# Seven block products for the left multiplication of two gated steps, scalings on ScalarE, and nine units in flight, in a four-layer graph kernel

## The chip, the cores and the metric

The kernel runs on one core of a Trainium2 chip. The metric is the device time of one execution in microseconds (us); less is better. The core has four engines that matter here: TensorE (PE; its weight loads are listed apart as PEld), VectorE (DVE), ScalarE (ACT) and GpSimd (POOL). SyncE (SP) issues most of the DMA transfers. Every engine works through its own instructions in a fixed order and waits at semaphores for the others.

## What is computed

Input x has 64 graphs of 256 nodes with 128 features in float32; one adjacency matrix adj (256 x 256, zeros and ones, symmetric) serves all. Four layers follow each other, each wrapped as x = layernorm(x + layer(x)). Cut to its core, the reference is:

```python
# layer 0: attention, softmax over axis 1, plus x @ self_weight
h = x @ others_weight
e = u1[:, idx1] + u2[:, idx2]; e = where(e >= 0, e, 0.1 * e)
out = softmax(where(adj > 0, e, NEG_BIG), axis=1) @ h + x @ self_weight
# layer 1: attention with leaky_relu(., 0.2) over adj + eye, then elu
h = x @ W; h_prime = softmax(masked(e_src + e_dst)) @ h; out = elu(h_prime)
# layer 2: five gated steps
for _ in range(5):
    m_in = einsum('nm,bmd->bnd', adj, h); m_out = einsum('nm,bmd->bnd', adj, h)
    av = concatenate([m_in, m_out], -1); u3 = h @ u3_w.T
    z = sigmoid(av @ w3_w.T + u3); r = sigmoid(av @ w4_w.T + u3)
    hv = tanh(av @ w5_w.T + (r * h) @ u5_w.T); h = (1 - z) * h + z * hv
# layer 3: x, adj x, adj^2 x, adj^3 x (twice) times seven weight matrices
y = einsum('bnik,iok->bno', stack(powers of adj on x), weight_1)
```

The change touches the products adj @ h of layer 2, the layernorms, and the scalings of the two attentions.

## The kernel before, in words

*Units and tiles.* Two graphs form a unit (UB = 2), so there are 32 units (NU). A unit's activations are 128 x 512 tiles: 128 partitions, and in the free dimension four blocks of 128, g = 2 b + c for graph b and node half c. "Node major" means nodes on the partitions, "feature major" features on them.

*Order of the work.* The functions `layer0` to `layer3` do not issue instructions. They hand tasks to `Plan.add` (L76), each with its engine, a priced duration in ns, and the cells (buffers) that it reads and writes. `Plan.run` (L103) then walks through time: whenever an engine is free it takes, among the tasks whose inputs are ready in the plan, the one with the smallest key. The key (`first`, L860) is the unit's number times PERIOD plus the task's due time, and the due time stretches the chain of a unit's tasks by PACE (PACE_GATED in layer 2). The order so found is emitted engine by engine, and the chip keeps it, whatever its own durations are. LANES = 8 units are open at once, each with its own set of buffers (`lane_cells`, L248); a unit that ends frees its lane for the unit eight further on. The eight PSUM banks are handed out by the plan as well: the first writer of a bank takes one, and it is free again when the last user has ended.

*Layer 0* (L564): products of x with weights (L582), scores (L613, L617), softmax by Exp on ACT (L627), the division by the softmax's sum applied to h on DVE (L631), then the self product (L644) and the attention product (L649) in one bank per graph. *Layer 1* (L662): scores by Prelu on ACT (L668), Exp (L671), mask (L672), attention product (L679), weight product (L692), division by the sum on DVE (L696, L697), elu (L704 to L712). *Layernorm* (L534): statistics on DVE (L541), variance plus eps (L543), the power -1/2 on POOL (L546), then four scalings of a 128 x 128 block each on DVE (L551 for layer 0, whose mean is zero by construction, L555 for the other three).

*Layer 2* (L724), per step: the left product, `left` (L716). It multiplies each node-major block of h, as weights, with the 128 x 256 half of the transposed adjacency that belongs to its node half, two blocks accumulating per graph: four products of 256 columns (L720) into one bank, feature major. ACT copies the bank to m (L736). Five products of 512 columns follow (L740): u3 with h and w4 with m give r, w5 with m, w3 minus w4 with m give z, u5 with r h. ACT evaluates the gates (L749, L756, L765), DVE combines them (L751, L763, L767, L769). The new h is feature major, and the next step needs it node major: for most units a 32 x 32 block transposition on DVE (L777, L790) and a trip through DRAM (L780 to L798) turn it, in a permuted order of nodes that `adjTp` absorbs; this is called far (`far`, L479). Units 0 and 1 in their first steps and the last two units use transposes on PE instead (L802).

*Layer 3* (L817): one left product, two sets of weight products (L833), a copy on ACT (L837), and the product with adj squared (L840), then the last layernorm and the transfer of the output.

*Start.* The first LANES units are loaded node major in one transfer each and turned on PE (L487); later units come in four transfers and are turned on DVE (L569). Units below DIRECT_ROWS spread their row of scores over the partitions with PE transposes (L530) and four small products (L607); the others send the rows through DRAM (L514, L518).

Of the kernel before, what the change touches and what calls it, by code (L numbers as in the profile page):

```python
# [17 lines left out]
LANES = 8  # L18
LEAD = 10
BANKS = 8  # L20
BL = 32
FIRST_FAR = {0: 2, 1: 2}
# [4 lines left out]
PACE = 2.1  # L27
PACE_GATED = 1.56
HOLD = 80
DIRECT_ROWS = 4  # L30
# [27 lines left out]
class Plan:  # L58
# [17 lines left out]
    def add(self, eng, ns, fn, reads=(), writes=(), after=(), wait=0, group=None, dma=False):  # L76
        t = Task(eng, ns, fn, self.unit, wait, dma or eng == "sp")
        for c in reads:
            t.deps.update(c.writers)
            c.readers.append(t)  # L80
        for c in writes:
            if c.bank and not c.writers:
                t.takes.append(c)
            if group is None or c.group is not group:
                c.waits = {w for o in (c, *c.over) for w in (*o.writers, *o.readers)} - {t}
                c.writers, c.readers, c.group = [], [], group
            t.deps.update(c.waits)
            c.writers.append(t)
        t.deps.update(after)
        t.deps.discard(t)  # L90
        for c in {id(c): c for c in (*reads, *writes) if c.bank}.values():
            c.users += 1
            t.banks.append(c)
        t.step = self.step = self.step + 1
        t.layer = self.layer
        t.rank = self.rank
        self.tasks.append(t)
        return t
# [90 lines left out]
def kernel(  # L189
# [101 lines left out]
    def load_x(u, by="sp"):  # L291
        z = lanes[u % LANES]["m"]
        if u < LANES:
# [48 lines left out]
    add(DVE, 60, lambda: nc.vector.memset(nhalf.ap, -0.5), (), (nhalf,))  # L342

# [106 lines left out]

    plan.rank = R3
# [82 lines left out]
    def layernorm(u, L, pairs, swap=False, centred=False):  # L534
# [11 lines left out]
        add(POOL, 1050, lambda: nc.gpsimd.tensor_tensor(rstd.ap, ve.ap, nhalf.ap, op=ALU.pow), (ve, nhalf), (rstd,))  # L546
        for k, (c, view) in enumerate(pairs):
            for j in range(2):
                b, ch = (j, k) if swap else (k, j)
                if centred:  # L550
                    add(DVE, 260, lambda k=k, j=j, b=b, ch=ch, view=view: nc.vector.tensor_scalar(  # L551
                        X[u].ap[:, b, ch, :], view()[:, j, :], rstd.ap[:, 2 * k + j : 2 * k + j + 1], 1.0,
                        op0=ALU.mult, op1=ALU.add), (c, rstd), (X[u],), group=xs)
                    continue
                add(DVE, 260, lambda k=k, j=j, b=b, ch=ch, view=view: nc.vector.tensor_scalar(  # L555
                    X[u].ap[:, b, ch, :], view()[:, j, :], st.ap[:, k, 3 * j + 1 : 3 * j + 2],
                    rstd.ap[:, 2 * k + j : 2 * k + j + 1], op0=ALU.subtract, op1=ALU.mult), (c, st, rstd), (X[u],), group=xs)
# [6 lines left out]
    def layer0(u, L):  # L564
        xT, z = L["xT0"], L["m"]
        if u < LANES:
# [49 lines left out]
        for b in range(UB):  # L616
            add(DVE, 260, lambda b=b: nc.vector.tensor_scalar_add(ev[:, b, :, P:N], neg0.ap[:, :, P:N], d.ap[:, b : b + 1]),  # L617
                (d, neg0), (e,), group=es)
# [7 lines left out]
        for g in range(G):  # L626
# [4 lines left out]
        add(DVE, 700, lambda: nc.vector.tensor_mul(  # L631
            h.ap[:, :, 0 : D + 2], h.ap[:, :, 0 : D + 2],
            rs.ap.rearrange("p (g o) -> p g o", o=1).to_broadcast([P, G, D + 2])), (h, rs), (h,))
# [28 lines left out]
    def layer1(u, L):  # L662
# [22 lines left out]
        for b in range(UB):  # L685
# [5 lines left out]
            for ic in range(NC):  # L691
# [5 lines left out]
            add(DVE, 350, lambda b=b, r=r, ov=ov: nc.vector.tensor_mul(  # L697
                gd(hp.ap)[:, b * NC : (b + 1) * NC, :], ov()[:, :, 0:D], r.to_broadcast([P, NC, D])), (ps_o, rs), (hp,), group=parts)
# [24 lines left out]

    def layer2(u, L):  # L724
        h, ht = turned(u, L, -1), X[u]
        for step in range(STEPS):
            ps_m = bank()
            for b in range(UB):
# [6 lines left out]
            m = L["m"]  # L735
            add(ACT, 500, lambda ps_m=ps_m: nc.scalar.copy(m.ap, ps_m.ap), (ps_m,), (m,))  # L736
# [163 lines left out]
```

## Time and profile before

| What | us |
|---|---|
| median of three runs | 1425.21 (1424.90 to 1425.53) |
| the profiled execution's own time | 1424.90 |
| its span, first to last instruction | 1423.0 |
| PE busy in the span | 1414.7 |
| DVE busy | 1119.5 |
| ACT busy | 729.3 |
| POOL busy | 140.8 |

The profile is one execution. A row of instructions reads: line, engine, operation, output <- input with sizes, how often; then busy time in us and the mean duration of one in ns; then the engine's idle time just before them and who ended it. A row of waits reads: engine and line that waited <- who released it: us in total, times, longest us. A row of the stretches reads: the stretch, its length, the busy time of PE, PEld, DVE, ACT and POOL with the count of instructions, then the granted clock of TensorE, the DMA share and GB/s. A row of the chain reads: start, us, what. An fp32 product is two PE records.

### The profile page before, as it was taken

Reading aid. Unit: us, or ns where it says so; the run is one execution under the profiler, and the core shown is the slowest. Engines: PE = TensorE matmul, PEld = TensorE weight load, DVE = VectorE, ACT = ScalarE, POOL = GpSimd, SP = SyncE. Lnnn points to the kernel's source line nnn. Section 1 sums busy time; section 2 is a strip of 40 time slices with the busy share of each in tenths; the row PEclk is TensorE's granted clock in tenths of the full one; section 3 lists DMA queues with packets and bytes.
Section 4 is the critical chain, followed back from the end, with each engine's and each line's share of the span. In section 5 each row is a group of like instructions: output and inputs, shape, how many; then the busy total and the mean of one; then the engine's idle time right before and its main releaser. Section 6 shows DMA issues by size and latency. Waiting matters only on the chain.

```text
span 1423.0 us, 18501 instructions
## 1 busy us (share of the span) xinstructions
PE 1414.7 (99%) x5661; PEld 958.7 (67%) x5661; DVE 1119.5 (79%) x2598; ACT 729.3 (51%) x1403; POOL 140.8 (10%) x134
## 2 busy tenths in 40 slices
PE   9999999999999999999999999999999999999998
PEld 8766666766666666667666667666766666667666
DVE  7977967888778887788877888888977767688554
ACT  5657445455455455555445554556454454455432
POOL 0110100110001110101110011100100101011001
PEclk9999999999999999999999999999999999999999
DMA  3114553545455444555445554444554454455101
GB/s 101 24 47 103 121 116 93 119 103 112 106 110 127 104 106 103 123 109 116 107 97 112 119 114 115 106 98 112 119 113 97 98 119 106 93 113 127 42 23 38
DMA packets 518099, 142.63 MB, mean 100 GB/s; under 512 B 447216, under 2 KB 484336, under 8 KB 518000
## 3 DMA queue, kind: packets, MB, share of 16 engines
q1 hardware_dynamic: 517200, 140.92, 44.1%
q8 instruction: 46, 0.75, 0.2%
q14 instruction: 53, 0.43, 0.1%
q10 hardware_dynamic: 800, 0.52, 0.1%
HBM read 78.73 MB, written 62.62 MB: 99 GB/s over the span
## 4 chain that ended last, share of the span: by engine, by line
PE 98%; DVE 1%; issue 0%; ACT 0%; POOL 0%; POOLq 0%; DVEq 0%
PE ps L740 48%; PE ps L720 23%; PE ps L833 8%; PE ps L649 4%; PE ps L679 4%; PE ps L840 4%; PE ps L692 2%; PE ps L644 2%; PE ps L582 2%; PE ps L802 0%; PE ps L487 0%; PE ps L336 0%; PE ps L530 0%; DVE x L555 0%; DVE st L541 0%
## 5 line engine op out<-in xcount | busy, mean ns | idle before, releaser
L740 PE MATMUL ps<-m,gT 128*128 128x512 f32 x960 | 456.1, 592 | 0.0
L740 PEld LDWEIGHTS ps<-m,gT 128*128 128x128 f32 x960 | 179.0, 190 | 152.0 <-issue 130.4
L546 POOL TENSOR_TENSOR rstd<-ve,nhalf 128x4 f32<-128x4 f32 x128 | 140.1, 1096 | 1277.5 <-DVE ve L543 1190.7
L720 PE MATMUL ps<-adjTp,ht 128*128 128x256 f32 x936 | 244.0, 379 | 0.0
L720 PEld LDWEIGHTS ps<-adjTp,ht 128*128 128x128 f32 x936 | 174.0, 190 | 65.3 <-issue 42.9
L749 ACT ACTIVATE e<-ps,bias 128x512 f32<-128x512 f32 x160 | 109.3, 684 | 155.8 <-PE ps L740 155.6
L756 ACT ACTIVATE e<-ps,bias 128x512 f32<-128x512 f32 x160 | 109.4, 685 | 120.2 <-PE ps L740 120.1
L740 PE MATMUL ps<-e,u5T 128*128 128x512 f32 x320 | 161.7, 592 | 0.0
L736 ACT COPY m<-ps 128x512 f32<-128x512 f32 x160 | 92.8, 583 | 118.9 <-PE ps L720 109.8
L765 ACT ACTIVATE p<-ps,bias 128x512 f32<-128x512 f32 x160 | 109.5, 685 | 84.7 <-PE ps L740 82.2
L767 DVE SCALAR_TENSOR_TENSOR p<-e,p 128x512 f32<-128x512 f32 x160 | 109.7, 687 | 39.1 <-ACT p L765 38.5
L720 PE MATMUL ps<-adjT,x 128*128 128x256 f32 x512 | 133.4, 379 | 0.0
L720 PEld LDWEIGHTS ps<-adjT,x 128*128 128x128 f32 x512 | 96.3, 190 | 49.3 <-issue 35.9
L751 DVE SCALAR_TENSOR_TENSOR e<-e,xT 128x512 f32<-128x512 f32 x96 | 65.4, 686 | 48.1 <-ACT e L749 45.2
L740 PE MATMUL ps<-xT,gT 128*128 128x512 f32 x192 | 98.1, 593 | 0.2 <-DVE xT L769 0.2
L740 PEld LDWEIGHTS ps<-e,u5T 128*128 128x128 f32 x320 | 59.7, 190 | 37.3 <-issue 29.1
L668 ACT ACTIVATE e<-m,esd 128x256 f32<-128x256 f32 x112 | 78.8, 757 | 0.0
L751 DVE SCALAR_TENSOR_TENSOR e<-e,p 128x512 f32<-128x512 f32 x64 | 43.9, 686 | 39.3 <-ACT e L749 39.3
L541 DVE BATCH_NORM_STATS2 st<-ps 128x6 f32<-128x256 f32 x128 | 51.3, 421 | 28.9 <-PE ps L840 14.5
L763 DVE SCALAR_TENSOR_TENSOR p<-e,xT 128x512 f32<-128x512 f32 x64 | 43.5, 680 | 37.2 <-ACT e L756 37.1
L679 PE MATMUL ps<-p,x 128*128 128x256 f32 x256 | 69.2, 379 | 0.3 <-DVE p L672 0.3
L649 PEld LDWEIGHTS ps<-ht,p 128*128 128x128 f32 x512 | 64.2, 190 | 5.7 <-issue 4.3
(149 smaller groups left out, 2116.7 us busy)
## 6 DMA issues: line engine op xcount, KB each, us to landing
hb<-p SPq DMA_DIRECT2D x176, 256.0 KB, 2.3
ht<-hb SPq DMA_DIRECT2D x468, 64.0 KB, 2.6
xT<-hb SPq DMA_DIRECT2D x236, 64.0 KB, 2.6
m<-row SPq DMA_DIRECT2D x56, 256.0 KB, 3.8
hb<-p SPq DMA_DIRECT2D x120, 64.0 KB, 1.8
ht<-hb SPq DMA_DIRECT2D x30, 256.0 KB, 2.7
out_dram<-x SPq DMA_DIRECT2D x29, 256.0 KB, 2.3
m<-in_x_dram SPq DMA_DIRECT2D x96, 64.0 KB, 2.5
```

The lines of the kernel that those rows point to most:

```text
L546: add(POOL, 1050, lambda: nc.gpsimd.tensor_tensor(rstd.ap, ve.ap, nhalf.ap, op=ALU.pow), (ve, nhalf), (rstd,))
L649: add(PE, mm_ns(D + 2), lambda b=b, ic=ic, kc=kc, yv=yv: nc.tensor.matmul(yv()[:, ic, :], p.ap[:, b * NC + kc, ic * P : (ic + 1) * P], h.a ...
L679: add(PE, mm_ns(N), lambda b=b, jc=jc: nc.tensor.matmul(ps_x.ap[:, b * N : (b + 1) * N], X[u].ap[:, b, jc, :], p.ap[:, b * NC + jc, :], st ...
L720: add(PE, mm_ns(N), lambda b=b, mc=mc: nc.tensor.matmul(ps.ap[:, b * N : (b + 1) * N], lhs(b, mc), mat.ap[:, mc, :], start=(mc == 0), stop ...
L736: add(ACT, 500, lambda ps_m=ps_m: nc.scalar.copy(m.ap, ps_m.ap), (ps_m,), (m,))
L740: add(PE, mm_ns(T), lambda: nc.tensor.matmul(ps.ap, w(), rhs.ap, start=start, stop=stop, skip_group_check=True), (c, rhs), (ps,))
L749: add(ACT, 600, lambda ps_g=ps_g, up=up: nc.scalar.activation(r.ap, ps_g.ap, AF.Tanh, bias=bias2.ap[:, 1:2], scale=0.5 / up), (ps_g, bias2 ...
L751: add(DVE, 600, lambda h=h: nc.vector.scalar_tensor_tensor(r.ap, r.ap, 1.0, h.ap, op0=ALU.add, op1=ALU.mult), (r, h), (r,))
L756: add(ACT, 600, lambda ps_g=ps_g, up=up: nc.scalar.activation(z.ap, ps_g.ap, AF.Tanh, bias=bias2.ap[:, 0:1], scale=0.5 / up), (ps_g, bias2 ...
L765: add(ACT, 600, lambda ps_v=ps_v, up=up: nc.scalar.activation(v.ap, ps_v.ap, AF.Tanh, bias=bias2.ap[:, 2:3], scale=1 / up), (ps_v, bias2), ...
L767: add(DVE, 600, lambda: nc.vector.scalar_tensor_tensor(v.ap, z.ap, 1.0, v.ap, op0=ALU.add, op1=ALU.mult), (v, z), (v,))
L833: add(PE, mm_ns(N), lambda k=k, src=src, c=c, b=b: nc.tensor.matmul(view(c)[:, :, b, :], bn(src.ap)[:, b, c * P : (c + 1) * P], w3.ap[:, k ...
```

## The change

Four things change together.

1. In steps 3 and 4 of layer 2, where the layout is far, `left_fast` takes the place of `left` and of the copy on ACT. Seen as 2 x 2 blocks of 128 x 128, the four products of 256 columns are eight block products; Strassen's scheme in Winograd's form makes do with seven. Three operand sums of h's blocks are formed on DVE, the sums of the adjacency's blocks once at the start (`adjTf`), the first product is copied to SBUF by ACT, and four DVE sums make m from the two banks x and y.
2. For units from 4 on (TIGHT), the layernorms' four scalings, layer 0's add of d and division, and layer 1's division go from DVE to ACT, one activation for each block with its scale or bias read from a column. Where the mean isn't zero a small DVE instruction forms minus mean times rstd first.
3. Nine units are open at once instead of eight; nine are loaded directly (XDIRECT), three instead of four have direct rows; PACE is 2.6.
4. In the plan, later writers of a bank wait for the first.

```diff
-LANES = 8
+LANES = 9
+FAST = (3, 4)
+NORM = (0, 1, 2, 3)
+SCALES = True
+TIGHT = 4
-PACE = 2.1
+PACE = 2.6
-DIRECT_ROWS = 4
+DIRECT_ROWS = 3
+XDIRECT = 9
...
+            if c.bank and c.writers:
+                t.deps.add(c.writers[0])
...
+    ones = cell("ones", [P, 1])
+    add(DVE, 60, lambda: nc.vector.memset(ones.ap, 1.0), (), (ones,))
...
+    adjTf = cell("adjTf", [P, 2 * NC, N])
...
+    add(DVE, 420, lambda: nc.vector.tensor_copy(adjTf.ap[:, 0:NC], adjTp.ap), (adjTp,), (adjTf,))
+    for out, (i, op, j) in {4: (1, ALU.subtract, 0), 6: (3, ALU.add, 1), 5: (6, ALU.subtract, 0)}.items():
+        add(DVE, 250, lambda out=out, i=i, op=op, j=j: nc.vector.tensor_tensor(block(out), block(i), block(j), op=op),
+            (adjTf,), (adjTf,))
+    add(DVE, 250, lambda: nc.vector.tensor_scalar_mul(block(5), block(5), -1.0), (adjTf,), (adjTf,))
+    add(DVE, 250, lambda: nc.vector.tensor_add(block(7), block(5), block(2)), (adjTf,), (adjTf,))
...
+        by_act = u >= TIGHT and plan.layer in NORM
+        if by_act and not centred:
+            add(DVE, 120, lambda: nc.vector.scalar_tensor_tensor(
+                ve..., st... , -1.0, rstd..., op0=ALU.mult, op1=ALU.mult), (st, rstd), (ve,))
...
+                shift, col = (ones, slice(0, 1)) if centred else (ve, at)
+                if by_act:
+                    add(ACT, 300, lambda ...: nc.scalar.activation(
+                        X[u].ap[:, b, ch, :], view()[:, j, :], AF.Identity, bias=shift.ap[:, col], scale=rstd.ap[:, at]),
+                        (c, shift, rstd), (X[u],), group=xs)
...
+            if SCALES and u >= TIGHT:
+                add(ACT, 370, lambda b=b: nc.scalar.activation(
+                    ev[:, b, :, P:N], neg0.ap[:, :, P:N], AF.Identity, bias=d.ap[:, b : b + 1]), (d, neg0), (e,), group=es)
...
+        for g in range(G if SCALES and u >= TIGHT else 0):
+            add(ACT, 270, lambda g=g: nc.scalar.activation(
+                h.ap[:, g, 0 : D + 2], h.ap[:, g, 0 : D + 2], AF.Copy, scale=rs.ap[:, g : g + 1]), (h, rs), (h,), group=hq)
...
+            for c in range(NC if SCALES and u >= TIGHT else 0):
+                add(ACT, 290, lambda b=b, c=c, ov=ov: nc.scalar.activation(
+                    gd(hp.ap)[:, b * NC + c, :], ov()[:, c, 0:D], AF.Copy, scale=rs.ap[:, b * NC + c : b * NC + c + 1]),
+                    (ps_o, rs), (hp,), group=parts)
...
+    def left_fast(src, blk, mat, s, p1, m):
+        four = gd(s.ap)
+        add(DVE, 360, lambda: nc.vector.tensor_sub(
+            four[:, 0:2], blk(slice(2, 3)).to_broadcast([P, 2, D]), blk(slice(0, 4, 3))), (src,), (s,), group=ss)
+        add(DVE, 220, lambda: nc.vector.tensor_sub(four[:, 2:3], four[:, 1:2], blk(slice(0, 1))), (src, s), (s,), group=ss)
+        add(DVE, 220, lambda: nc.vector.tensor_add(four[:, 3:4], four[:, 2:3], blk(slice(1, 2))), (src, s), (s,), group=ss)
+        x, y = bank(), bank()
+        def one(ps, at, lhs, k, c, cells):
+            add(PE, mm_ns(P), lambda: nc.tensor.matmul(
+                ps.ap[:, at * P : (at + 1) * P], lhs(), mat.ap[:, k, c * P : (c + 1) * P], start=True, stop=True,
+                skip_group_check=True), (*cells, mat), (ps,), group=four)
+        one(x, 0, a(0), 0, 0, (src,))
+        add(ACT, 280, lambda: nc.scalar.copy(p1.ap[:, 0:P], x.ap[:, 0:P]), (x,), (p1,))
+        one(x, 1, a(1), 1, 0, (src,))
+        one(y, 3, a(3), 3, 1, (src,))
+        one(y, 1, sm(0), 3, 0, (s,))
+        one(y, 0, sm(1), 2, 0, (s,))
+        one(x, 2, sm(2), 2, 1, (s,))
+        one(y, 2, sm(3), 1, 1, (s,))
+        add(DVE, 400, lambda: nc.vector.tensor_tensor(
+            mv[:, 0:4:3], pv(x)[:, 1:3], p1... .to_broadcast([P, 2, P]), op=ALU.add), (x, p1), (m,))
+        add(DVE, 400, lambda: nc.vector.tensor_tensor(
+            mv[:, 1:3], pv(y)[:, 0:2], mv[:, 3:4].to_broadcast([P, 2, P]), op=ALU.add), (y, m), (m,))
+        add(DVE, 240, lambda: nc.vector.tensor_add(mv[:, 3:4], pv(y)[:, 0:1], mv[:, 2:3]), (y, m), (m,))
+        add(DVE, 400, lambda: nc.vector.tensor_add(mv[:, 1:3], pv(y)[:, 2:4], mv[:, 1:3]), (y, m), (m,))
...
+            fast = step in FAST and far(u, step - 1)
+            ps_m = None if fast else bank()
+            if fast:
+                left_fast(ht, lambda g: gd(ht.ap)[:, g], adjTf, L["r"], L["z"], m)
```

## The prediction

> **What bounds the kernel now.** I read first the busy shares with the chain that ended last, then TensorE's own waits, then stretches of time, then pieces of the chain, then rows of instructions.
>
> ```profile
> PE 1414.7 (99%) x5661; PEld 958.7 (67%) x5661; DVE 1119.5 (79%) x2598; ACT 729.3 (51%) x1403; POOL 140.8 (10%) x134
> ...
> PE 98%; DVE 1%; issue 0%; ACT 0%; POOL 0%; POOLq 0%; DVEq 0%
> ```
>
> TensorE (PE) is busy nearly throughout, and 98% of the chain is PE. A busy share can hide gaps, since matmul ends are modelled; so I look at what PE waited for, in total:
>
> ```profile
> PE ps L336 <- POOL ident masks.py:199: 1.4, 1, 1.4
> PE ps L679 <- DVE p L672: 0.3, 1, 0.3
> PE ps L607 <- ACT ht L585: 0.3, 1, 0.3
> PE ps L740 <- DVE xT L769: 0.2, 1, 0.2
> ```
>
> 2.2 us in all. By stretches (length; then PE, PEld, DVE, ACT, POOL busy):
>
> ```profile
> 70.00:80.00 10.00, 10.00 (x51) 7.33 (x50) 6.70 (x17) 9.87 (x29) 0.00 (x0) 1.00 0.01 2
> ...
> 400.00:700.00 300.00, 300.00 (x1183) 202.55 (x1182) 246.67 (x561) 154.81 (x299) 30.59 (x28) 1.00 0.50 111
> ...
> 1410.00:1423.00 13.00, 7.05 (x32) 5.46 (x30) 7.00 (x21) 0.74 (x2) 3.02 (x3) 0.94 0.22 62
> ```
>
> Only the start and the last 6 us have PE idle. The chain's pieces (start, us, what) give what one PE record costs without its overlap:
>
> ```profile
> 76.99 6.87 PE ps L740 x16
> ...
> 151.80 4.75 PE ps L720 x22
> ...
> 512.00 0.45 PE ps L644 x4
> ...
> 513.32 1.79 PE ps L649 x16
> ...
> 555.20 0.45 PE ps L644 x4
> ```
>
> So 6.87/16 = 0.429 us for 512 columns, 4.75/22 = 0.216 for 256, 1.79/16 = 0.112 for 130; each fp32 product is two such records. Per unit the source issues 50 records of L740, 80 of 256 columns (48 of L720, 8 of L679, 16 of L833, 8 of L840) and 40 of about 130 (L582, L644, L649, L692): 21.5 + 17.3 + 4.5 = 43.2 us. The same place recurs one unit later, after 555.20 - 512.00 = 43.2 us. In mid-run the time is PE's work and nothing else.
>
> **What the Trainium skill says.** (1) "TensorE: Matmul & The Clock Gate", section "Back-to-back issue gap", says that small products fall behind the column count because of their weight load, and "LDWEIGHTS" prices a load of 128 columns at 107 ns. The trace's 130-column record with new weights takes 112 ns, 2 x 130/2.4 + 3.6, so the load is just covered there; at 128 columns it nearly ties. (2) "PSUM — Partial Sum Buffer", section "PSUM bank collisions raise a hardware error", wants engines kept apart by bank, not by address; no wait in the old trace shows it, but the new program has it (below). (3) "ScalarE: Activation LUTs", section "Table sets", puts copy and identity in every set: no table reloads from the new ScalarE work. The trace has one load for exp, tanh, Prelu and copies together, and the built program keeps one.
>
> **The change, part by part.** Rows for other durations:
>
> ```profile
> L736 ACT COPY m<-ps 128x512 f32<-128x512 f32 x160 | 92.8, 583 | 118.9 <-PE ps L720 109.8 <-DVE ve L543 2.8 <-issue 1.9
> ...
> L837 ACT COPY e<-ps 128x256 f32<-128x256 f32 x64 | 23.6, 371 | 77.4 <-PE ps L833 76.5
> ...
> L551 DVE TENSOR_SCALAR x<-ps,rstd 128x128 f32<-128x128 f32 x128 | 38.9, 342 | 4.6 <-POOL rstd L546 4.6
> ...
> L697 DVE TENSOR_TENSOR ht<-ps,rs 128x256 f32<-128x256 f32 x64 | 24.6, 413 | 0.4
> ```
>
> *Seven products.* They replace L720 where the step is 3 or 4 and the layout is far: units 0 to 29, 60 unit steps. Removed: 8 records of 256 columns, 8 x 0.216 = 1.728 us. Added: 14 of 128 columns; between 112 (130 columns) and the line through 130 and 256 columns that is 0.110 us, so 1.544. Saved 0.184 x 60 = 11.0 us of PE. Bounds: if a record ran no faster than the 0.112 of 130 columns 9.6 us, if it needed columns alone (0.107) 13.8.
>
> *Direct rows and loads.* Unit 3 no longer makes its rows on PE: 8 transposes (0.44 us for 4 in L802's pieces) and 8 records of L607 (0.62 us for 6 at 10.69 us) go, 1.7 us; unit 8, now loaded directly, adds 4 transposes, 0.4. Its load is one transfer instead of four; unit 3 adds seven on SP in the start (rows out and back), behind which stand the rows of units 4 and later. A row lands in 3.8 us (issues of m<-row); the built order has the products of units 0 to 2 ahead of unit 3's next, more than 10 us, so nil; 4 us if that cover were gone. Net -1.2 us of PE. In all PE has 12.2 us less.
>
> *Nine units, new priorities, the plan's bank rule.* These only reorder. No stall goes, since PE never lacked work in mid-run; a ninth unit has nothing to fill there, and its price is in the start, below.
>
> *VectorE.* A fast step adds three operand sums (415 + 282 + 282 ns, from L697's width and the 282 of 128-wide tensor_tensor at L427) and four result sums (3 x 413 + 290): 2.5 us, 150 us in 60. Setup adds 1.8, the negated means 84 x 0.16 = 13.5. Off it, for 28 units: 16 scalings of 0.34 to 0.40, two adds of 0.35 (L617), one of 0.70 (L631), two of 0.41 (L697): 7.9 us, 221 in all. Net -56: 1063 us, 75%. No bound.
>
> *ScalarE.* Per fast step a 583 copy becomes a 128-wide one, 265 by the line through 371 and 583: -19 us. Per unit of 28 come 16 + 2 + 4 + 4 activations; no row shows one 128 wide. "ScalarE: Activation LUTs" prices 186 ns + 0.833 per column and 93 for each pointer operand, with 93 overlapped; L749's 685 at 512 columns against its 706 agrees. That is 0.48 with two pointers, 0.39 with one: 11.8 us a unit for 26 of them, 329 us, or 262 less the overlaps. ACT then stands at 972 to 1039 us, 69 to 74%. No bound over the run.
>
> *The start.* Units 4 to 8 together now put layers 0 and 1's share, about 6.2 us each or 31 us, on ACT within the first 100 us, where it was busy 61 of 100 (summed over its stretches) and, in the stretch shown, 9.87 of 10. So ACT nearly fills there, and PE may wait for it. In the built order PE also has 38.3 us of work before its first 512-column product where it had 40.4. I put +1.5 us on the start; bounds -1 (VectorE, over 90% busy from 20 to 70 us, is relieved) and +5.
>
> *New waits in mid-run.* m is now four dependent VectorE sums instead of one copy. Pricing the built order with the records above, PE has other work between the last of the seven products and m's first use of 2.0 us at least, 3.0 in nine of ten, median 3.9; before it was 0.9, 1.7 and 2.2. Needed are 0.16 of matmul latency (592 - 429) and 1.53 of sums, against 0.16 + 0.58 before: the margin grows from 1.0 to 1.3 at the tenth. The first product's copy to p1 stands in ACT's queue; because of the shared bank the sixth product waits for it on PE in 43 of 60 steps, with all of PE queued behind it. Between lie 0.43 us at least, median 1.1; needed are 0.16 + 0.27 and hops. Cost nil where ACT is free, up to 0.4 in the 17 under 0.9 us if ACT is inside a 685 ns activation: 0 to 7 us, and I take 0.5. The first sum waits on VectorE for products and copy; behind it stand other units' gate operations (L751, L767), which PE's L740 needs. The scalings on ACT wait for POOL's 1.1 us power through VectorE; behind them are tanh and m copies. Both have the cover named.
>
> *The end.* After PE's last record the last layernorm runs alone: four DVE scalings in 1.36 us become four of ACT, 0.48 + 3 x 0.39 = 1.65, plus a 0.16 sum and a hop: +0.5.
>
> **Sum.** The profiled execution took 1424.9 us, span 1423.0 and 1.9 around it, 0.3 under the median of 1425.2. Span: 1423.0 - 12.2 + 1.5 + 0.5 + 0.5 = 1413.3. Outside the profile that is 1425.2 - 9.7 = 1415.5.
>
> **Rivals.** *The start gains.* VectorE's relief removes what PE loses there beyond its first 1.4 us (0.6 in L679's and L607's waits, and what modelled ends hide) and the ACT load costs nothing: 1425.2 - 12.2 - 1 + 0.5 = 1412.5, down to 1410. For: VectorE's 90%. Against: ACT's 9.87. *Waits eat most.* ACT's crowded start (5) and the p1 copy (3 to 7) together give back 8 to 12 us: 1421 to 1426. For: ACT rises by a third. Against: only two of those 43 waits have under 0.6 us of other PE work before them. *Slower.* VectorE runs behind the plan's order, which prices its 687 ns operations at 600; in fast steps m or the operand sums then arrive late and PE stands at the first product with m. It decides at 12/60 = 0.2 us a step; with VectorE 2 us late the median margin of 2.2 is used up and half of the steps lose about 1 us: 60 x 0.5 = 30, so 1443. For: seven more ordered VectorE operations a step. Against: VectorE gets lighter, and at 79% it cost PE 0.2 us after the start. *The change does not take hold:* excluded, the built program has 420 products of 128 columns more for 240 of 256 fewer.
>
> **How the numbers follow.** Forecast 0.64, start gains 0.08, waits eat most 0.15 (half of it still over 0.2% faster), slower 0.13. About 0.2%, 2.85 us, is what a measurement here can tell from no change. Faster 0.64 + 0.08 + 0.08 = 0.80, same 0.07, slower 0.13. The range 1411 to 1422 leaves out the slower case and the worse half of the third, 0.20.
>
> **What would show it.** Right: the recurring place comes after 43.2 - 0.4 = 42.8 us in mid-run; 14 records of the new line in 1.54 us; PE's waits in mid-run under 2 us; ACT near 70%, DVE near 75%. Wrong: PE waits named after the p1 copy or the sums, PE gaps between 40 and 100 us that end with ACT, or 128-column records of over 0.123 us (1.728/14), where the saving is gone.

## The result, and the profile after

The changed kernel takes 1424.83 us (1424.48 to 1426.96, four runs) against 1425.37 (1424.90 to 1426.04) for the kernel before beside it: a ratio of 0.9999, with a 95% interval from 0.9982 to 1.0016. No change of the time can be told. The forecast was 1415.5. The profiled execution took 1424.77 us, its span is 1422.9, and the page gives the engines' busy time and the chain's shares:

```profile
PE 1408.2 (99%) x6009; PEld 959.7 (67%) x6009; DVE 1082.7 (76%) x2521; ACT 954.1 (67%) x2132; POOL 141.5 (10%) x134
...
PE 93%; ACT 2%; DVE 1%; DMA 1%; SPq 1%; issue 1%; POOLq 0%; ACTq 0%; DVEq 0%
```

PE has 348 records more and is busy 6.5 us less, VectorE is lighter and ScalarE a third heavier, all as intended; yet the span is the same, and PE's share of the chain is 93% where it was 98%. The chain in mid-run (start, us, what) shows that the seven products do their work:

```profile
514.21 0.67 PE ps L788 x6
...
515.74 0.89 PE ps L788 x8
...
557.09 0.67 PE ps L788 x6
...
558.62 0.89 PE ps L788 x8
```

14 records of 128 columns take 0.67 + 0.89 = 1.56 us, 0.111 each, and the same place comes again after 557.09 - 514.21 = 42.88 us, where the kernel before needed 43.2. So time is lost elsewhere. Stretches of the changed kernel, two of which the prediction shows of before (length; PE, PEld, DVE, ACT, POOL busy with counts; clock, DMA share, GB/s):

```profile
70.00:80.00 10.00, 10.00 (x36) 5.95 (x35) 9.18 (x23) 10.00 (x25) 1.19 (x1) 1.00 0.07 26
400.00:700.00 300.00, 299.63 (x1272) 203.86 (x1271) 234.36 (x538) 213.30 (x486) 31.23 (x28) 1.00 0.50 111
1000.00:1250.00 250.00, 247.12 (x959) 157.01 (x958) 186.65 (x405) 158.44 (x348) 18.48 (x18) 1.00 0.47 104
```

PE is idle for 2.9 us between 1000 and 1250 us. The kernel before has no idle time there:

```profile
1000.00:1250.00 250.00, 250.00 (x920) 161.07 (x919) 190.99 (x419) 124.68 (x228) 20.38 (x19) 1.00 0.48 105
```

PE's waits over the whole run (who waited for whom: us in total, times, longest), after:

```profile
PE ps L843 <- ACT e L852: 1.6, 4, 0.8
PE ps L344 <- POOL ident masks.py:199: 1.4, 1, 1.4
PE ps L725 <- DVE rs L671: 1.3, 1, 1.3
PE ps L619 <- ACT e L859: 0.9, 1, 0.9
...
PE ps L843 <- ACT p L868: 0.4, 1, 0.4
...
PE ps L690 <- ACT p L868: 0.3, 1, 0.3
PE ps L843 <- DVE m L821: 0.2, 1, 0.2
```

Two of these are worth learning to read. L619 is a product of layer 0 with its weights and L690 layer 0's self product: neither reads what a gate of layer 2 (L859, L868) writes. What ties them to a gate is the PSUM bank that the gate's tanh is the last to read; PE waits for a bank. Of the 3.8 us listed after 100 us, 1.6 are such waits (L619, L690, and L843 behind L868, the gate of another unit). Another 1.6, the first row, are not: there a unit's own gate product waits until its own tanh (L852) has read the same bank, and no other product is ready. The largest wait for a bank, in order of time on PE (start, us, what, idle time before it and its releaser):

```profile
1027.89 1.02 PE L843 MATMUL ps<-e,u5T 128*128 128x512 f32 x2
1028.75 0.62 PE L619 MATMUL ps<-wx,xT 128*128 128x133 f32 x4
1030.23 0.72 PE L619 MATMUL ps<-wx,xT 128*128 128x133 f32 x4 [0.87 <-ACT e L859]
```

The listed waits add up to some 8 us, but they see only idle time beyond the modelled end of a product, which for 512 columns lies 592 - 429 = 163 ns after the next can start. So I count gaps another way: from the start of each PE record to the start of the next, less the price of the record when it runs back to back (0.429 us at 512 columns, 0.216 at 256, 0.114 at 133, 0.110 at 128). The span is then the first record's start (1.36 us in all), the priced records, the gaps, and what follows the last record's start (that record, 0.2 us, stands in two of these). Gaps near zero, some of them negative, are the rounding of these prices, and nearly 2 us of the first 100 are no waits in any kernel: the first records of 256 columns take 0.43 us there. For every kernel of this study, gaps by stretch:

| kernel | median us | ratio, 95% interval | PE records | gaps, all | to 100 us | 100 to 1000 | 1000 to 1250 | rest | last record to end |
|---|---|---|---|---|---|---|---|---|---|
| before | 1425.4 | | 1410.5 | 5.1 | 4.1 | 0.3 | 0.4 | 0.2 | 6.4 |
| changed | 1424.83 | 0.9999 [0.9982, 1.0016] | 1398.3 | 16.5 | 7.0 | 3.2 | 5.8 | 0.6 | 7.0 |
| e1 products | 1433.29 | 1.0057 [1.0044, 1.0069] | 1399.5 | 24.4 | 5.4 | 12.2 | 6.3 | 0.5 | 6.4 |
| e2 scalings | 1430.37 | 1.0037 [1.0024, 1.0049] | 1410.5 | 9.8 | 4.9 | 4.2 | -0.1 | 0.8 | 6.8 |
| e3 nine units | 1429.05 | 1.0027 [1.0017, 1.0038] | 1409.2 | 9.9 | 5.6 | 1.2 | 2.4 | 0.7 | 6.7 |
| e4 products, nine units | 1428.53 | 1.0024 [1.0014, 1.0034] | 1398.3 | 21.4 | 8.8 | 4.0 | 6.9 | 1.8 | 6.7 |
| e5 products, scalings | 1433.46 | 1.0057 [1.0044, 1.0070] | 1399.5 | 23.8 | 8.4 | 11.5 | 3.0 | 0.9 | 6.9 |
| e6 scalings, nine units | 1430.13 | 1.0032 [1.0019, 1.0044] | 1409.2 | 9.9 | 5.5 | -0.3 | 3.2 | 1.5 | 7.0 |
| e7 ScalarE's prices | 1427.99 | 1.0017 [1.0011, 1.0024] | 1398.3 | 19.5 | 9.7 | 2.4 | 6.1 | 1.3 | 7.4 |
| e8 bank for p1 | 1433.51 | 1.0061 [1.0048, 1.0075] | 1398.3 | 24.5 | 7.0 | 7.0 | 9.0 | 1.4 | 7.0 |
| e11 sums alone | 1446.55 | 1.0153 [1.0139, 1.0167] | 1409.2 | 27.3 | 6.5 | 4.0 | 6.1 | 10.8 | 7.0 |
| e12 banks alone | 1429.11 | 1.0031 [1.0021, 1.0041] | 1409.2 | 9.7 | 6.8 | -0.5 | 2.4 | 1.1 | 7.0 |
| e10 pace alone | 1428.47 | 1.0027 [1.0017, 1.0037] | 1398.3 | 19.7 | 6.7 | 10.6 | 1.8 | 0.7 | 7.4 |
| e9 m first, other pace | 1420.14 | 0.9962 [0.9949, 0.9974] | 1398.3 | 10.6 | 8.7 | 1.4 | 0.2 | 0.3 | 7.0 |
| e18 m first, own pace | 1423.68 | 0.9990 [0.9982, 0.9998] | 1398.3 | 15.8 | 9.3 | 6.0 | 0.1 | 0.4 | 7.0 |
| e13 m first, four products | 1430.20 | 1.0035 [1.0023, 1.0048] | 1409.2 | 10.2 | 8.8 | 1.0 | 0.3 | 0.2 | 7.0 |
| e14 before, other pace | 1434.48 | 1.0063 [1.0051, 1.0076] | 1410.5 | 14.3 | 4.8 | 1.2 | 0.9 | 7.4 | 6.4 |
| e15 m first, set-up later | 1417.25 | 0.9944 [0.9932, 0.9957] | 1398.3 | 10.6 | 9.0 | 1.2 | 0.1 | 0.3 | 6.9 |
| e17 m first, four rows | 1418.43 | 0.9951 [0.9937, 0.9965] | 1400.0 | 9.3 | 6.0 | 2.9 | 0.1 | 0.3 | 7.0 |
| e16 four rows, other pace | 1416.18 | 0.9936 [0.9923, 0.9950] | 1400.0 | 6.1 | 4.9 | 0.8 | 0.1 | 0.3 | 7.1 |

Gaps belong to the profiled execution, the median to all runs; e9's profile is the fastest of its five (1418.76 us). From before to changed: records 1410.5 - 1398.3 = 12.2 us less, gaps 11.4 more, the end 0.6 more. All of the expected gain in PE's work is there, and all of it is given back as time in which PE finds nothing to do.

### The profile page after: what moved, and what is told of

Same layout as the page of the kernel before. It is cut to its first block, busy times and chain, and to the rows that moved or that the text cites. A ratio compares the mean times of both kernels' runs of the same rounds, so it can differ in the third digit from the quotient of the medians.

```text
span 1422.9 us, 19902 instructions
## 1 busy us (share of the span) xinstructions
PE 1408.2 (99%) x6009; PEld 959.7 (67%) x6009; DVE 1082.7 (76%) x2521; ACT 954.1 (67%) x2132; POOL 141.5 (10%) x134
## 4 chain that ended last, share of the span: by engine, by line
PE 93%; ACT 2%; DVE 1%; DMA 1%; SPq 1%; issue 1%; POOLq 0%; ACTq 0%; DVEq 0%
PE ps L843 46%; PE ps L771 16%; PE ps L936 8%; PE ps L788 6%; PE ps L695 4%; PE ps L943 4%; PE ps L725 4%; PE ps L738 2%; PE ps L690 2%; PE ps L619 2%; DMA m<-in_x_dram 1%; ACT e L714 1%; DMA ht<-hb 1%; PE ps L905 0%; SPq L886 0%
## 5 line engine op out<-in xcount | busy, mean ns | idle before, releaser
L843 PE MATMUL ps<-m,gT 128*128 128x512 f32 x960 | 462.0, 594 | 2.4 <-ACT e L852 1.6
L843 PEld LDWEIGHTS ps<-m,gT 128*128 128x128 f32 x960 | 172.7, 190 | 138.3 <-issue 109.1
L852 ACT ACTIVATE e<-ps,bias 128x512 f32<-128x512 f32 x160 | 109.5, 686 | 107.6 <-PE ps L843 106.9
L843 PE MATMUL ps<-e,u5T 128*128 128x512 f32 x320 | 162.7, 593 | 0.0
L859 ACT ACTIVATE e<-ps,bias 128x512 f32<-128x512 f32 x160 | 110.1, 688 | 51.4 <-PE ps L843 50.3
L868 ACT ACTIVATE p<-ps,bias 128x512 f32<-128x512 f32 x160 | 109.8, 688 | 41.1 <-PE ps L843 39.4
L771 PE MATMUL ps<-adjT,x 128*128 128x256 f32 x512 | 136.2, 379 | 0.0
L839 ACT COPY m<-ps 128x512 f32<-128x512 f32 x100 | 58.2, 582 | 95.2 <-PE ps L771 94.9
L771 PEld LDWEIGHTS ps<-adjT,x 128*128 128x128 f32 x512 | 94.7, 190 | 37.2 <-issue 25.7
L771 PE MATMUL ps<-adjTp,ht 128*128 128x256 f32 x456 | 118.1, 379 | 0.4 <-DMA ht<-hb 0.4
L771 PEld LDWEIGHTS ps<-adjTp,ht 128*128 128x128 f32 x456 | 85.3, 190 | 31.3 <-issue 19.9
L843 PE MATMUL ps<-xT,gT 128*128 128x512 f32 x192 | 97.7, 593 | 0.4 <-ACT p L868 0.4
L843 PEld LDWEIGHTS ps<-e,u5T 128*128 128x128 f32 x320 | 58.6, 190 | 47.7 <-issue 35.1
L525 DVE STREAM_TRANSPOSE p<-x 128x512 f32<-128x512 f32 x59 | 65.6, 1113 | 16.9 <-ACT x L584 10.8
L788 PEld LDWEIGHTS ps<-adjTf,e 128*128 128x128 f32 x480 | 62.6, 191 | 15.1 <-issue 7.8
L725 PE MATMUL ps<-p,x 128*128 128x256 f32 x256 | 69.5, 380 | 1.3 <-DVE rs L671 1.3
```

Source lines behind the costliest of these rows:

```text
L725: add(PE, mm_ns(N), lambda b=b, jc=jc: nc.tensor.matmul(ps_x.ap[:, b * N : (b + 1) * N], X[u].ap[:, b, jc, :], p.ap[:, b * NC + jc, :], st ...
L771: add(PE, mm_ns(N), lambda b=b, mc=mc: nc.tensor.matmul(ps.ap[:, b * N : (b + 1) * N], lhs(b, mc), mat.ap[:, mc, :], start=(mc == 0), stop ...
L788: add(PE, mm_ns(P), lambda: nc.tensor.matmul(ps.ap[:, at * P : (at + 1) * P], lhs(), mat.ap[:, k, c * P : (c + 1) * P], start=True, stop=True,
L843: add(PE, mm_ns(T), lambda: nc.tensor.matmul(ps.ap, w(), rhs.ap, start=start, stop=stop, skip_group_check=True), (c, rhs), (ps,))
L852: add(ACT, 600, lambda ps_g=ps_g, up=up: nc.scalar.activation(r.ap, ps_g.ap, AF.Tanh, bias=bias2.ap[:, 1:2], scale=0.5 / up), (ps_g, bias2 ...
L859: add(ACT, 600, lambda ps_g=ps_g, up=up: nc.scalar.activation(z.ap, ps_g.ap, AF.Tanh, bias=bias2.ap[:, 0:1], scale=0.5 / up), (ps_g, bias2 ...
```

## The experiments

### The parts, alone and in pairs (e1 to e6)

```diff
-FAST = (3, 4)      # e2, e3, e6: FAST = (), and no adjTf
-NORM = (0, 1, 2, 3)    # e1, e3, e4: NORM = (), SCALES = False
-LANES = 9          # e1, e2, e5: LANES = 8, PACE 2.1, DIRECT_ROWS 4, XDIRECT 8
```

> The seven products alone; scalings stay on VectorE, eight units, old priorities. PE's work falls by 11.0 us. If the late ScalarE scalings caused the lost time: PE gaps stay near before's 5 us, 1414 to 1416 us. If the products' own waits (copy to p1, four sums) caused it: gaps of 14 to 17 us, 1424 to 1427. If nine units and the new priorities did: 1414 to 1416.

> The scalings on ScalarE alone; old left products, eight units, old priorities. PE's work is unchanged. If the scalings caused the lost time: gaps of 13 to 17 us, 1432 to 1437 us. If the products' waits or the nine units did: 1424 to 1427.

> Nine units, nine direct loads, three direct rows and PACE 2.6 alone. PE's work falls by 1.2 us. If nine units and the priorities caused the lost time: 1430 to 1436 us. If the scalings or the products did: 1423 to 1426.

> After, with the scalings back on VectorE. PE's work is after's, 1398.3 us. If the scalings caused the lost time: gaps fall from 16.5 to about 5 to 7 us, 1413 to 1416 us. If the products' own waits or the nine units did: 1423 to 1426. VectorE rises to 86%, so if VectorE was about to be the next to be late, PE waits named after VectorE's sums appear, 1418 to 1425.

> Products and scalings, but eight units, PACE 2.1 and four direct rows. If the products' own waits cost most and the scalings win part back by making VectorE lighter: between products alone (1433.3) and after (1424.8), about 1427 to 1430. If a lane more and the priorities were what made after bearable: over 1430. If nine units were the cost: under 1422.

> Scalings and nine units, old left products. PE's work 1409.2 us. If the lost time belongs to the seven products: 1424 to 1428, with gaps of 5 to 9 us. If it comes with every new order of the instructions, whatever the edit: again 1428 to 1431, as with each part alone.

Each part alone is slower than the kernel before: +8.1 us (products), +5.2 (scalings), +3.9 (nine units). The products save 11.0 us of records in every pairing, and cost more gaps in every pairing: e1 against before 24.4 - 5.1 = 19.3, e5 against e2 14.0, e4 against e3 11.5, the changed kernel against e6 6.6. The scalings or the nine units cost 4.7 to 4.8 us of gaps, alone or together. e1 and e4 came out slower than any branch of their expectations, and e2 and e3 between two branches; e6 met the branch by which every new order of the instructions costs something, whatever the edit. So the loss can't be put down to one part, and its place isn't shown yet. The fourth part, the plan's bank rule, stays in all of these runs. Adding it alone to the source of the kernel before leaves the plan's order as it was, so it is no cause there.

### Two guesses at the place (e7, e8)

e7 gives ScalarE's operations in the plan the pitches that the trace shows (for example 370 ns for a scaling that the plan prices at 300, 495 for an Exp at 400). e8 gives the first of the seven products a bank of its own, so that the sixth needn't wait for the copy to p1, the wait that the prediction had named.

```diff
-add(ACT, 300, lambda ...: nc.scalar.activation(   # e7, and four more prices
+add(ACT, 370, lambda ...: nc.scalar.activation(
...
-x, y = bank(), bank()                             # e8
+x, y, w = bank(), bank(), bank()
-one(x, 0, a(0), 0, 0, (src,))
+one(w, 0, a(0), 0, 0, (src,))
```

> After, with the plan's prices of ScalarE's activations set to their measured start to start times (Exp with its sum 495 for 400, Prelu 650 for 600, layernorm scaling 370 for 300, add of d 420 for 370, division 300 for 270). If PE waits because ScalarE runs behind the plan in such bursts: gaps fall from 16.5 to 6 to 10 us, 1414 to 1419. If the products' bank wait or VectorE's sums cause it: 1423 to 1427.

> After, with the first product in a bank of its own, so that no later product waits on PE for ScalarE's copy to p1; three banks instead of two per fast step. If that wait is the cost: gaps fall by 4 to 8 us, 1417 to 1421. If not: 1423 to 1428, more if banks are short.

Neither helps: gaps of 19.5 and 24.5 us against 16.5, and e7's median is above both of its branches. In e8 two products of the seven are listed behind L800 all the same (0.7 us): they take the bank that the copy to p1 has just left. Nothing here speaks for a late ScalarE or for the shared bank of p1 as the cause; but both edits draw a new order too, so a small part of either could hide. That a third bank goes with 8 us more of gaps was the first sign that banks are scarce.

### The sums against the second bank (e11, e12)

Undone from the changed kernel each time are the seven products. e11 keeps the operand sums, the copy to p1 and the result sums around the four old products in one bank; m's values are then not the product. e12 keeps the two banks and has no sums: one graph to a bank, two half copies on ScalarE. e6 has neither. In e11 all four products wait for the operand sums, where three of the seven didn't, so its way to m is longer than the changed kernel's (30.5 against 27.3 us, table below).

```diff
-one(x, 0, a(0), 0, 0, (src,))  ...  one(y, 2, sm(3), 1, 1, (s,))
+for b in range(UB):                               # e11, then the sums from x
+    for mc in range(NC):
+        add(PE, mm_ns(N), ... x ... blk(b, mc) ... adjTp ..., (src, adjTp, s), (x,))
...
-left_fast(ht, ..., adjTf, L["r"], L["z"], m)      # e12
+for b in range(UB):
+    ps_h = bank()
+    left(ps_h, ht, b, ..., adjTp)
+    add(ACT, 300, ... nc.scalar.copy(bn(m.ap)[:, b], bn(ps_h.ap)[:, b]), (ps_h,), (m,), group=...)
```

> The changed kernel with its sums but not its seven products: steps 3 and 4 take the four old products of 256 columns in one bank, behind the three operand sums and ahead of the copy of the first block and the four result sums. m's values are then not the product adj h; PE has the old work, one bank is held. PE records 1409.2 us as with scalings and nine units alone (gaps 9.9 there). Theory 1 in its form 'the longer chain of a fast step is what starves PE': gaps 18 to 27, median 1437 to 1446. Theory 3 (second bank): gaps 8 to 12, median 1428 to 1433. Theory 2: gaps 12 to 18, the same VectorE work being there, median 1431 to 1438.

> The changed kernel with the second bank but neither sums nor seven products: in steps 3 and 4 the four old products go to two banks, one for each graph, and ScalarE copies each half to m. PE records 1409.2 us; gaps 9.9 with scalings and nine units alone. Theory 1 (chain): gaps 8 to 12, median 1428 to 1432. Theory 3 (second bank): gaps 17 to 25, median 1436 to 1445. Theory 2: gaps 8 to 12, since VectorE has less to do.

The second bank alone costs nothing (gaps 9.7 against e6's 9.9). With the sums alone, and PE's old work, they are 27.3, just above what the first theory expected (18 to 27); from 100 to 1250 us that is 10.1, as in the changed kernel (9.0), against 2.9 in e6. PE's waits in e11 after the first 100 us:

```profile
PE ps L918 <- DMA xT<-hb: 4.7, 1, 4.7
PE ps L825 <- ACT e L841: 1.6, 2, 0.8
PE ps L825 <- ACT e L834: 1.0, 3, 0.3
PE ps L825 <- DVE p L525: 0.8, 1, 0.8
PE ps L771 <- ACT e L841: 0.8, 1, 0.8
...
PE ps L825 <- DVE m L803: 0.3, 1, 0.3
```

Only 0.3 us of that names m's last sum (L803). The rows of L825 behind L834 and L841 and of L771 are a unit's next product behind a gate, or another unit's left product (L771) behind a gate's bank: the sums seldom make PE wait at m, they leave it with too little else. A part of e11's gaps, 10.8 us, lies after 1250 us, where the changed kernel has 0.6. Most of it is the first row, near the end of the run, where the transfer of a turned block comes late and the records of 256 columns behind it take some 0.43 us each instead of 0.216 (granted clock from 1429 to 1437 us 0.59). Without the 10.8, 16.5 are left against e6's 8.4.

### The bank that the product with h opens (e9, e10, e18, e13)

From the source's order of tasks and the trace's times I took how long each bank is held, from the first PE record that writes it to the end of the last instruction that reads it; and how long a unit (4 to 25) needs in steps 3 and 4 from the end of h's block transposition to the end of m's last writer. ps_g and ps_v are the two banks of a gated step:

| kernel | ps_g held, mean us | ps_v held, mean us | banks held, 300 to 1000 us | 1000 to 1250 us | transposition to m, mean us |
|---|---|---|---|---|---|
| before | 21.7 | 8.5 | 5.6 | 6.5 | 20.8 |
| e6 | 23.6 | 9.2 | 6.1 | 7.1 | 25.6 |
| changed | 23.8 | 8.8 | 6.4 | 7.1 | 27.3 |
| e11 | 24.9 | 8.6 | 6.6 | 7.0 | 30.5 |
| e10 | 23.2 | 8.1 | 6.4 | 7.1 | 24.6 |
| e18 | 9.6 | 10.4 | 5.4 | 5.7 | 25.6 |
| e9 | 9.3 | 9.9 | 5.5 | 5.8 | 24.3 |
| e13 | 9.5 | 10.3 | 4.8 | 5.6 | 22.9 |

There are eight banks. ps_g is opened by the product with h, which is ready at once, and is then held while h is turned through DRAM and m is formed; a longer way to m should hold it longer, and a ninth unit can add one more such bank. The table bears out the second more than the first: ps_g is held as long in e6, without the seven products, as in the changed kernel (23.6 and 23.8 us), and 4.8 of the 6.5 us by which the way to m grows are there in e6 too. So I exchanged the two products: m opens the bank, h follows. Number and kind of the instructions stay the same.

```diff
-product(ps_g, lambda: gT.ap[:, 3], gT, h, True, False)
-product(ps_g, lambda: gT.ap[:, 1], gT, m, False, True)
+product(ps_g, lambda: gT.ap[:, 1], gT, m, True, False)
+product(ps_g, lambda: gT.ap[:, 3], gT, h, False, True)
...
-PACE = 2.6             # e9, e10, e13; not e18
-PACE_GATED = 1.56
+PACE = 3.0
+PACE_GATED = 1.45
```

e10 has the new pace without the exchange, e18 the exchange without the pace, e13 both with FAST = (), that is with the four old products. The pace was picked as one at which the planner's own order left PE little idle.

> The changed kernel with the first two products of ps_g exchanged: the product with m opens the bank and the product with h follows, so that the bank isn't held while h is turned and m is formed; PACE 3.0 and PACE_GATED 1.45, chosen with it. The instructions are otherwise the same in number and kind. Theory 1 (the order runs short of ready work for PE: a fast step's chain is longer, and all that time a bank opened by the product with h is held, so that other units' products find no bank): PE records 1398.3 us as in the changed kernel, gaps 4 to 8 us instead of 16.5, median 1412 to 1417. Theory 2 (VectorE and ScalarE are late on the chip against the plan, whatever the banks do): gaps stay at 14 to 20, median 1422 to 1429. Theory 3 (it is the second bank of the seven products): as theory 2, since both banks are held as long as before.

> The changed kernel with PACE 3.0 and PACE_GATED 1.45 and nothing else, the control for the run with the product of m first. Theory 1: another order with the same bank times, so gaps no smaller, 15 to 22 us, median 1424 to 1431. If the pace is what helps there, gaps 4 to 8 and 1412 to 1417 here too.

> The changed kernel with the two first products of ps_g exchanged and nothing else; PACE 2.6, PACE_GATED 1.56 as in the changed kernel. If the shorter hold of the bank is all that is needed: gaps after 100 us fall from 9.6 to under 3, median 1416 to 1419.5. If the order's draw matters as well as the hold: the gaps of 1000 to 1250 us (5.8) go, but 3 to 7 us stay elsewhere, median 1420 to 1426.

> The kernel with the product of m first, at the same PACE 3.0 and PACE_GATED 1.45, but with the old four products and the copy on ScalarE in steps 3 and 4 (the sums of the adjacency at the start stay). PE records 1409.2 us. Theory 1 (what ate the products' saving was the shortage of ready work and banks, and it is now gone): gaps as in the kernel with the product of m first, 8 to 11 us, so 1427 to 1430, and the seven products are worth 7 to 11 us between the two. Rival (the product of m first is worth the same with and without the seven products, and these still lose most of their saving): gaps 3 to 6, 1421 to 1425, the products worth under 5.

In the source e9 and e10 differ by the exchange alone: 1420.14 against 1428.47 us, 8.3 us; the plan draws another order with it. e9's gaps of 10.6 lie between what the first theory (4 to 8) and the others (14 to 20) had expected. e9 has gaps of 1.9 us after the first 100 us instead of the changed kernel's 9.6, and no wait of PE is listed there any more. e10's list after 100 us begins

```profile
PE ps L771 <- ACT m L839: 2.5, 9, 0.5
PE ps L843 <- DVE m L821: 1.0, 2, 0.8
```

L771, a left product, doesn't read m; it waits for the bank that the copy L839 of another unit empties. Nine such waits are listed, and eight gaps of 0.41 us lie between 541 and 845 us, one in each period of some 43.4 us. The Trainium skill ("Perfetto Trace Analysis", section "Optimization Strategy") says of a gap that repeats on the engine that should be saturated that it can mean too little SBUF or PSUM for the next tile; here it did: each of the nine waits follows the last reader of the bank that the product takes, and with the shorter hold of e9 they are gone. The section "Matmul Optimizations" there asks that all eight banks be put to use. The 20 traces add the other side for 1000 to 1250 us: at a mean of 6.4 to 6.6 banks held, gaps are -0.1 to 0.9 us (before, e2, e14); at 6.7 to 7.2 they are 1.8 to 9.0 (the other eleven with h first); at 5.6 to 5.8, 0.1 to 0.3 (the six with m first). Within the eleven the count doesn't order them. I also followed each gap of over 0.1 us from 100 to 1250 us back to the instruction that ended last, among those whose results the product reads and those that last read the bank it takes. Gaps behind a bank come to 0.1 us at most in before, e2 and e14, to 1.0 to 8.2 us in the eleven (2.0 in the changed kernel), and to none in the six but e18 (0.5). From 300 to 1000 us the count of banks orders the kernels less well. The stretches of e9 beside those of the changed kernel:

```profile
400.00:700.00 300.00, 299.94 (x1270) 203.81 (x1270) 230.28 (x541) 211.43 (x479) 30.98 (x28) 1.00 0.50 112
1000.00:1250.00 250.00, 250.00 (x978) 159.98 (x977) 193.04 (x423) 160.81 (x340) 20.81 (x18) 1.00 0.48 106
```

e13 shows to whom the gain belongs. With four products and the same exchange and pace the time is 1430.20 us, no better than e6's 1430.13: exchange and pace together are worth nothing there, and beside e13 the seven products are worth 1430.2 - 1420.1 = 10.1 us at last, of 10.9 in records. The rival of that run, by which the exchange helps both alike, falls. In e13 the gaps from 1000 to 1250 us do go (e6 3.2, e13 0.3), but the start's grow as much (5.5 to 8.8). One reason shows in the waits before 100 us: with m first, unit 0's gate product waits for the copy of m, 1.6 us in e9, e13 and e18 against 0.5 in the changed kernel.

e18 corrects the theory. The exchange alone removes the gaps from 1000 to 1250 us (5.8 to 0.1), but leaves 6.0 between 100 and 1000, although banks are as free as in e9, and adds 2.3 to the start. By the medians it is about 1 us faster than the changed kernel, and the intervals of the two ratios overlap. Its only listed waits after the start are these:

```profile
PE ps L788 <- ACT e L800: 0.7, 2, 0.5
PE ps L788 <- DVE e L781: 0.7, 1, 0.7
```

They are the p1 copy, and an operand sum. Banks alone are not the whole cause. I take it that with banks free the order of priority decides whether PE has something else to do while a fast step's chain runs; that is argued from e18 against e9 and not shown apart. Three orders with h first (changed, e7, e10) have gaps of 16.5, 19.5 and 19.7 us, three of the same products with m first (e9, e15, e18) 10.6, 10.6 and 15.8.

### The draw of the order, and the start (e14 to e17)

e14 is the kernel before with PACE 2.3 for 2.1. e15 is e9 with the six VectorE instructions of adjTf ranked behind the start (plan.rank = 4) and PACE 3.2, PACE_GATED 1.56. e16 is e9 with DIRECT_ROWS = 4, PACE 2.8, PACE_GATED 1.56 and PERIOD 42.5e3. e17 is e9 with DIRECT_ROWS = 4 alone.

```diff
-PACE = 2.1             # e14, kernel before
+PACE = 2.3
...
-DIRECT_ROWS = 3        # e16, e17
+DIRECT_ROWS = 4
...
+    plan.rank = 4      # e15, ahead of adjTf's six instructions
```

> The kernel before with PACE 2.3 instead of 2.1 and nothing else: another order of the same instructions. Theory 1: the order of before is a good draw, and any other costs some PE gaps: 8 to 12 us instead of 5.05, 1428 to 1433. If the order alone costs nothing: gaps 4 to 6, 1424 to 1427, and what the scalings alone and nine units alone lost needs another cause.

> The kernel with the product of m first, with the six VectorE instructions that form the adjacency's sums put behind the start in the plan's order, PACE 3.2 and PACE_GATED 1.56. If the start's extra gaps (8.7 us before 100 us, against 4.1 in the kernel before) come from VectorE doing the sums there: start gaps 5.5 to 7, mid-run gaps under 2, 1416.5 to 1419. If they come from the nine units' own work: start gaps 8 to 9.5, 1419 to 1422.

> The kernel with the product of m first, with DIRECT_ROWS 4 as in the kernel before (1.3 us of PE records more), PACE 2.8, PACE_GATED 1.56, PERIOD 42.5e3. If the start's extra gaps come from unit 3's rows going through DRAM: start gaps 5 to 7, mid-run gaps under 2, PE records 1399.6, 1417 to 1420. If not: start gaps 8 to 9.5, 1420.5 to 1423.

> The first kernel with the product of m first (PACE 3.0, PACE_GATED 1.45, PERIOD 43e3) with DIRECT_ROWS 4 instead of 3 and nothing else; PE records rise from 1398.3 to 1400.0 us. If unit 3's rows through DRAM cost the start its extra gaps: start gaps 4.5 to 6 instead of 8.7, median 1417 to 1419.5. If it was the other pace that helped the kernel with four rows: start gaps 8 to 9.5, median 1420.5 to 1423.

e14 costs the kernel before 9.1 us, more than expected, for one constant and no work: gaps of 14.3, 7.4 of them in the last 180 us. Its two largest waits are there:

```profile
PE ps L487 <- DVE x L555: 3.4, 1, 3.4
PE ps L802 <- DVE p L769: 1.6, 1, 1.6
```

Both are the last unit's own products behind its own VectorE results: this order leaves the unit alone at the end, with nothing beside it. The records behind the longer wait run slow (granted clock from 1417 to 1420.5 us 0.56). Between 100 and 1250 us e14 has 2.1 us of gaps, against 0.7 before. So a new order alone can cost 9 us, but what it cost here is the end, not the middle of the run; e14 doesn't explain the gaps of the changed kernel or of e3 and e6 there, and of two orders one can't say which is the usual one. e15's start gaps stay at 9.0, so adjTf's instructions are not what fills the start; it is faster than e9 in the median, but not in gaps. e17's fall from 8.7 to 6.0, for 1.7 us more of records and 1.5 more of gaps in mid-run: the rows of unit 3 through DRAM cost some 2.7 us of start there. e16 has another draw as well, start gaps of 4.9, and is the fastest: 1416.18 us, 9.2 less than before (ratio 0.9936, from 0.9923 to 0.9950). It is the changed kernel with m first, four direct rows and other constants; how much of its gain the exchange and the constants would bring to the kernel before, without the change, was not run. It has 6.1 us of gaps, and none to speak of here:

```profile
1000.00:1250.00 250.00, 250.00 (x991) 161.46 (x990) 191.59 (x424) 164.03 (x358) 18.18 (x17) 1.00 0.49 108
```

## Why the prediction was wrong

- *Seven products, direct rows and loads: right.* Records fell by 12.2 us, as the sum had it; 0.111 us for a record of 128 columns (0.110 forecast), the period 42.88 us (42.8 forecast), p1's copy 268 ns (265 forecast).
- *Nine units, new priorities, the plan's bank rule ("These only reorder. No stall goes"): wrong.* I asked whether a stall would go, and not whether one would come. PE was full in mid-run because the order nearly always had a ready product with a free bank; that is a property of the order, which the change draws anew. And the ninth unit was not free: without the seven products it already leaves 2.9 to 3.6 us of gaps between 100 and 1250 us (e6, e3; before 0.7), with the mean of banks held from 1000 to 1250 us up from 6.5 to 7.1 (e6).
- *New waits in mid-run (0.5 us, bounds 0 to 7): the step that failed.* It measured 2.9 us between 100 and 1000 and 5.4 between 1000 and 1250, 8.3 in all and beyond the bound. That is 7.8 of the 9.6 us by which the span of 1422.9 missed 1413.3; the start is 1.4 of them. The margin between a product and m's use, which I worked out, was right for what it asks: only 0.2 us of wait names m's last sum. But it took for granted that the other work in between is there. In the changed kernel it often isn't. For 1000 to 1250 us the runs show why: banks are taken by gates that wait for m, and where m opens the bank the gaps there are gone, in all six kernels. e11 against e12 points to the chain of sums, not the second bank, as what the seven products add; each is one order, so this is likely and not proven. For 100 to 1000 us the cause stays open.
- *The p1 copy: not here.* No listed PE wait of the changed kernel names L800, and a bank of its own went with more gaps (e8). In e18 the wait is listed, with 0.7 us.
- *The start (+1.5): too small.* It measured 7.0 - 4.1 = 2.9 us, inside its bounds, and not mainly where I looked: the largest new wait, 1.3 us, is unit 0's attention product of layer 1 (L725) behind VectorE, where the kernel before had 0.3; waits that end with ACT are 0.7. The price of nil for unit 3's rows was part of it: 2.7 us in e17 against e9. How much of that the changed kernel itself loses was not run.
- *The end (+0.5): right*, 0.6.
- *VectorE and ScalarE (1063 us; 972 to 1039): 1082.7 and 954.1, neither a bound, as forecast, but both off.* VectorE lost less than forecast, and ScalarE lies below its range. The scalings took 148 us from VectorE (e2), not 207: the sum of its instructions' durations fell by 204, but they overlap, and busy time counts an overlap once. On ScalarE they added 242 (e2), under the 262 of the estimate from the Trainium skill, "ScalarE: Activation LUTs", section "What ACT_TABLE_LOAD costs"; a scaling takes 0.46 to 0.49 us in the groups of L584, where the page's price comes to 0.48.
- *Rivals.* "Waits eat most" (1421 to 1426) named the right size by luck, since of its two places ScalarE's crowded start took 0.7 us in the listed waits and the p1 copy none. "Slower" by a late VectorE didn't come. The list of what would show it wrong held no line for PE waits behind another unit's gate, or behind a unit's own tanh with nothing else ready, which are most of what is listed after 100 us. Its gaps between 40 and 100 us that end with ACT came too, two waits of 0.5 and 0.2 us, and are in the start's 2.9.

What stays open: in 100 to 1000 us, how much is due to banks and how much to priorities (e18 leaves 6.0 us with free banks, e10 10.6 without); and what the exchange would do in the kernel before.

## What to carry over

When a change takes work off a saturated engine and lengthens a chain elsewhere, don't ask only whether the chain's result is in time; ask what keeps the saturated engine fed meanwhile, and which buffers stand open while the chain runs. A gap on PE that ends with an instruction whose data PE doesn't read is likely a wait for a bank, so look who read that bank last; let the operand that comes last open the accumulation, and check the start, where there may be nothing else to run meanwhile. Where an order is drawn from priorities, a change of work has to be compared over several draws, since one constant here moved the time by 9 us; and look where in the run a draw loses it before comparing.

## What was not expected of the hardware

- The 14 records of seven products of 128 columns, each with new weights, run at some 0.111 us a record (1.56 us for 14 in the chain): the weight load stays covered at 128 columns.
- Gaps below the modelled end of a product (163 ns) don't show in PE's busy share: e18 has 6.5 us of gaps after the first 100 us, and a wait list of 1.4.
- After waits of PE of 3.4 (e14) and 4.7 us (e11) near the end of the run, the records behind them took up to twice their time, with a granted clock of 0.56 to 0.59.
